# Router logits of a mixture-of-experts layer: from TensorE matmuls to products on VectorE and sums on ScalarE

## The chip, the cores and the metric

The kernel runs on one core of one Trainium2 chip. The core has five engines with an instruction queue each, and each queue is worked off in order: TensorE (PE, matmuls; its weight loads are listed as PEld), VectorE (DVE), ScalarE (ACT), GpSimd (POOL) and SyncE (SP, which here only issues transfers and reads table entries). Time is device time of one execution in microseconds. The kernel before takes 2452.55 us, the median of 3 runs (2449.38 to 2454.42).

## The reference

The inputs are a batch of 4 with 64 channels, 512 time steps and 64 variables; the model width is D = 256, and 16384 tokens come out. All is float32.

```python
h = tok(x, W)                    # patches of 16, stride 8, FFT, one linear map to D
x1 = layernorm(h)
a  = layernorm(x1)
q, k, v = a @ Wq.T + bq, a @ Wk.T + bk, a @ Wv.T + bv
mem_t = decay * mem_{t-1} + k_t * v_t        # a scan along the tokens
x2 = x1 + q * mem
h  = h + x2 + relu(layernorm(x2) @ W1.T + b1) @ W2.T + b2
tokens = layernorm(h)            # the expert layer's input
logits = tokens @ router_w.T     # 8 experts: the part that is changed
rw, re = top_k(softmax(logits), 2);  rw = rw / rw.sum(-1)
h = h + tokens + sum_e combine[:, e] * (gelu(tokens @ w1[e] + b1[e]) @ w2[e] + b2[e])
```

## The kernel before

Tokens go through in 32 blocks of 512, each held as four groups of 128 tokens (TT = 4) on the 128 partitions. The main loop runs over periods; period i works at three blocks at once: `new` (block i: embedding, layernorms, q/k/v and the scan), `mid` (block i-1: the MLP) and `old` (block i-2: routing). Between their parts stand up to four slots; a slot is one step over the queue of expert tiles of 256 gathered tokens, taken while more than 12 tiles (LEFT) wait, and in the last periods while any wait. The two last periods have no `new`, the very last no `mid` either; what is left of the tiles follows after them.

A period's program, in the order in which it is written: embed's first part (L258, ScalarE's copy into `ms` at L262); features2 of mid (transposes of `zz`, L213, and ScalarE's copies with scale, L221); the first half of embed (L269, VectorE's sum into `h` at L276, statistics at L184 and L185); features3 of old (transposes of `tok`, copies L215); embed's second half, then rstd on GpSimd (L191 to L196) and `zz` and `z` on VectorE (L200); slot A; eight mlp_in (L229 on TensorE, relu on ScalarE at L343), the first four with a group of old's logits after each (L385); slot B and choose after the fourth; features1 of new before the eighth; place, take and the differences `xd` of the next block (L246, L247); retention for two halves of the features (per half three products L229, `ks` on ScalarE at L298, and `kv`, the scan and `ret` on VectorE at L300 to L313); slot C; mlp_out for the first half (L351, VectorE L358); residual (transposes of `ret` L323, VectorE L326, rstd on GpSimd, `zz` at L200, two additions to `h` at L332 and L333); slot D; mlp_out for the second half, which ends with rstd on GpSimd, `tok` on VectorE (L200) and the addition to `h` at L365.

choose finds the two best experts of each token in some 13 tiny VectorE instructions (L404 to L420) and a power on GpSimd (L422). place counts, by two matmuls (L429), where each token's rows go, and writes them with eight indirect DMAs from GpSimd (L450). take turns the counts into tables of tiles, which SP reads. In a slot, TensorE transposes the tile after the next (turn, L572), multiplies one (enter, L581) and finishes the one before (leave, L598). ScalarE copies `xT` (L574) and applies gelu (L589, two instructions). VectorE makes `y` (L607 to L614), and GpSimd adds its rows into the output in DRAM by two indirect DMAs (L618); the adds of a tile wait for those of the tile before.

The order is written out by hand: on TensorE, VectorE, ScalarE and SP the instructions stand in the order of the program (`manual_schedule`); on GpSimd, too, they come out in that order here. The PSUM pools set further bounds: `p_mm` has four buffers and holds, one after another, the outputs of transposes into features, mlp_in, q, k, v, turn and enter; `p_tm` has three, for embed, residual, leave and mlp_out.

Of the kernel before, what the change touches and what calls it, by code (L numbers as in the profile page):

```python
# [12 lines left out]
F32 = mybir.dt.float32  # L13
I32 = mybir.dt.int32
AF = mybir.ActivationFunctionType
# [14 lines left out]
def vit_tower_kernel(  # L30
# [17 lines left out]
    D = wtok.shape[1]  # L48
    C = P // 2
    H = w1.shape[1]  # L50
    E = rw.shape[1]
    KD, KH = D // P, H // P
    J = STRIDE // 2
    TT = 4
# [69 lines left out]
    nc.sync.dma_start(out=w1_sb, in_=w1.rearrange("(k p) h -> p k h", p=P))  # L124
    w2_sb = const.tile([P, KH, D], F32)
    nc.sync.dma_start(out=w2_sb, in_=w2.rearrange("(k p) d -> p k d", p=P))
    rw_sb = const.tile([P, KD, E], F32)
    nc.sync.dma_start(out=rw_sb, in_=rw.rearrange("(k p) e -> p k e", p=P))
    mb2_sb = const.tile([P, D], F32)
    nc.sync.dma_start(out=mb2_sb, in_=mb2.partition_broadcast(P))  # L130
    rc = const.tile([P, 2, P], F32)
# [102 lines left out]
    class Block:  # L234
# [139 lines left out]
                    channel_multiplier=2,  # L374
                )

        def features3(self):
            self.tokT = one.tile([P, KD, BLK], F32, name="tokT")
            to_features(self.tokT, self.tok)

        def logits(self, t):
            if t == 0:
                self.lg = p_sm.tile([P, TT, E], F32, name="sm")
            for k in range(KD):
                nc.tensor.matmul(  # L385
                    self.lg[:, t, :],
                    lhsT=self.tokT[:, k, ts(t, P)],
                    rhs=rw_sb[:, k, :],
                    start=k == 0,
                    stop=k == KD - 1,  # L390
                )

        def choose(self):

            ps = self.lg
            shape = [P, TT, E]

            def wide(a):
                return a.unsqueeze(2).to_broadcast(shape)

            lg = small.tile(shape, F32, name="lg")
            top = small.tile([P, TT], F32, name="top")
            first_key = self.tok[:, :, FIRST]
            nc.vector.tensor_copy(lg, ps)  # L404
            nc.vector.tensor_reduce(top, lg, AX.X, ALU.max)
            nc.vector.tensor_tensor(lg, lg, wide(top), ALU.subtract)
            key = small.tile(shape, F32, name="key")
            self.oh = oh = small.tile([P, 2, TT, E], F32, name="oh")
            nc.vector.scalar_tensor_tensor(key, lg, 0.0, key0, ALU.is_equal, ALU.mult)
            nc.vector.tensor_reduce(first_key, key, AX.X, ALU.max)  # L410
            nc.vector.tensor_tensor(oh[:, 0], key, wide(first_key), ALU.is_equal)
            nc.vector.scalar_tensor_tensor(lg, oh[:, 0], -3.0e38, lg, ALU.mult, ALU.add)
            second = small.tile([P, TT], F32, name="second")
            nc.vector.tensor_reduce(second, lg, AX.X, ALU.max)
            nc.vector.tensor_tensor(key, lg, wide(second), ALU.is_equal)
            nc.vector.tensor_tensor(key, key, key0, ALU.mult)
            nc.vector.tensor_reduce(top, key, AX.X, ALU.max)
            nc.vector.tensor_tensor(oh[:, 1], key, wide(top), ALU.is_equal)
            self.both = small.tile(shape, F32, name="both")
            nc.vector.tensor_tensor(self.both, oh[:, 0], oh[:, 1], ALU.add)  # L420
            self.ex = small.tile([P, TT], F32, name="ex")
            nc.gpsimd.tensor_tensor(self.ex, euler, second, ALU.pow)  # L422
# [238 lines left out]
    with tc.manual_schedule(engines=MANUAL):  # L661
        xs[1] = load_x(1)
        blocks[0].differences(xs.pop(0))
        for i in range(NB + 2):
            new = blocks[i] if i < NB else None
            mid = blocks[i - 1] if 1 <= i <= NB else None
            old = blocks[i - 2] if i >= 2 else None
            embed = new.embed() if new else iter(())
            next(embed, None)
            if mid:  # L670
                mid.features2()
            next(embed, None)
            if old:
                old.features3()
            next(embed, None)
            slot(LEFT if new else 0)
            for m in range(KH):
                if mid:
                    mid.mlp_in(m)
                if old and m < TT:  # L680
                    old.logits(m)
                if m == TT - 1:
                    slot(LEFT if new else 0)
                    if old:
                        old.choose()
                if new and m == KH - 2:
                    new.features1()
            if not mid:
                slot(0)
            if old:  # L690
                take(old.i + 1, old, old.place())
            if i + 1 < NB:
                blocks[i + 1].differences(xs.pop(i + 1))
                if i + 2 < NB:
                    xs[i + 2] = load_x(i + 2)
            if new:
                for m in range(KD):
                    new.retention(m)
                slot()
            if mid:  # L700
                mid.mlp_out(0)
            if new:
                new.residual()
                slot()
            if mid:
                mid.mlp_out(1)
            if mid and not new:
                slot(0)
                slot(0)
# [84 lines left out]
```

## Time and profile before

| | |
|---|---|
| median of 3 runs | 2452.55 us |
| the profiled execution's own time | 2448.38 us |
| its span, first to last instruction | 2446.4 us |
| busy time: PE, DVE, POOL, ACT | 2298.4, 1347.3, 930.1, 556.7 us |
| mean granted TensorE clock | 0.979 |

The page counts an engine as busy while it executes; waits on semaphores are not busy time. The timeline lists instructions with start, duration, engine and line; brackets give the idle time ahead of an instruction and what ended it. A label such as `mm<-hT,w_sb` reads output first, then inputs. A float32 matmul shows as two records of matmul, so that a group of TensorE can list twice the count of the program.

### The profile page before, as it was taken

Reading aid. Unit: us, or ns where it says so; the run is one execution under the profiler, and the core shown is the slowest. Engines: PE = TensorE matmul, PEld = TensorE weight load, DVE = VectorE, ACT = ScalarE, POOL = GpSimd, SP = SyncE. Lnnn points to the kernel's source line nnn. Section 1 sums busy time; section 2 is a strip of 40 time slices with the busy share of each in tenths; the row PEclk is TensorE's granted clock in tenths of the full one; section 3 lists DMA queues with packets and bytes.
Section 4 is the critical chain, followed back from the end, with each engine's and each line's share of the span. In section 5 each row is a group of like instructions: output and inputs, shape, how many; then the busy total and the mean of one; then the engine's idle time right before and its main releaser. Section 6 shows DMA issues by size and latency. Waiting matters only on the chain. (4 is left out here: it accounts for less than half of the span.)

```text
span 2446.4 us, 29049 instructions
## 1 busy us (share of the span) xinstructions
PE 2298.4 (94%) x9740; PEld 1687.8 (69%) x9740; DVE 1347.3 (55%) x4111; ACT 556.7 (23%) x952; POOL 930.1 (38%) x845
## 2 busy tenths in 40 slices
PE   3999999999999999999999999999999999986673
PEld 2677666777777777777777777777777777665553
DVE  6566665565655555655555556555555665533221
ACT  0122222222222222222222222222222222221221
POOL 0022222344444334444443344444433444335444
PEclk8999999999999999999999999999999999998887
DMA  4021121333344343333443433334334333347674
GB/s 140 18 79 59 56 105 64 98 89 102 109 122 116 103 110 101 89 102 109 122 113 105 112 101 89 102 109 122 111 107 111 102 90 85 91 106 208 168 182 86
DMA packets 128181, 256.44 MB, mean 105 GB/s; under 512 B 14497, under 2 KB 88097, under 8 KB 123937
## 3 DMA queue, kind: packets, MB, share of 16 engines
q1 hardware_dynamic: 76864, 185.09, 23.3%
q0 software_dynamic: 51168, 69.50, 15.3%
q8 instruction: 77, 1.26, 0.2%
q14 instruction: 72, 0.58, 0.1%
HBM read 164.04 MB, written 90.50 MB: 104 GB/s over the span
## 5 line engine op out<-in xcount | busy, mean ns | idle before, releaser
L618 POOL DMA_INDIRECT out<-y,xg x270 | 426.1, 1578 | 587.6 <-DVE y L614 386.9
L229 PE MATMUL mm<-hT,w_sb 128*128 128x512 f32 x1024 | 478.3, 600 | 0.0
L351 PE MATMUL tm<-w_sb,aT 128*128 128x256 f32 x2048 | 453.0, 379 | 0.0
L351 PEld LDWEIGHTS tm<-w_sb,aT 128*128 128x128 f32 x2048 | 388.5, 190 | 54.9 <-issue 2.4
L450 POOL DMA_INDIRECT xbuf<-tok,row x256 | 314.4, 1228 | 238.1 <-DVE whole L506 161.5
L229 PE MATMUL mm<-hT,wqkv_sb 128*128 128x512 f32 x768 | 338.1, 596 | 0.1
L612 DVE TENSOR_TENSOR y<-tm,w 128x512 f32<-128x512 f32 x135 | 93.3, 691 | 382.8 <-PE tm L598 226.9
L229 PEld LDWEIGHTS mm<-hT,w_sb 128*128 128x128 f32 x1024 | 184.6, 190 | 158.4 <-issue 155.4
L581 PE MATMUL mm<-xT,w 128*128 128x256 f32 x1080 | 275.9, 401 | 3.5 <-DVE ret L313 2.3
L191 POOL TENSOR_SCALAR rstd<-mv 128x4 f32<-128x4 f32 x96 | 37.1, 387 | 635.8 <-DVE mv L185 635.8
L343 ACT ACTIVATE aT<-mm,vec 128x512 f32<-128x512 f32 x256 | 175.9, 687 | 395.2 <-PE mm L229 392.6
L229 PEld LDWEIGHTS mm<-hT,wqkv_sb 128*128 128x128 f32 x768 | 143.9, 191 | 169.6 <-issue 154.1
L598 PE MATMUL tm<-w,ge 128*128 128x256 f32 x1080 | 258.4, 383 | 0.0
L269 PE MATMUL tm<-weff,xd 128*128 128x256 f32 x1024 | 233.4, 382 | 8.5 <-DVE xd L246 8.5
L581 PEld LDWEIGHTS mm<-xT,w 128*128 128x128 f32 x1080 | 206.2, 201 | 34.6 <-DVE ret L313 9.2
L598 PEld LDWEIGHTS tm<-w,ge 128*128 128x128 f32 x1080 | 209.1, 194 | 29.9
L269 PEld LDWEIGHTS tm<-weff,xd 128*128 128x128 f32 x1024 | 191.1, 192 | 32.7 <-DVE xd L246 8.9
L574 ACT COPY xT<-mm 128x512 f32<-128x512 f32 x135 | 79.0, 585 | 531.3 <-PE mm L572 528.2
L589 ACT ACTIVATE ge<-mm,w 128x256 f32<-128x256 f32 x270 | 113.1, 470 | 182.7 <-PE mm L581 157.2
L572 PE MATMUL mm<-ident,xg 128*128 128x128 f32 x540 | 85.1, 282 | 64.9 <-DMA xg<-xbuf 64.8
L258 PE MATMUL tm<-wsum,xb 128*128 128x256 f32 x512 | 118.3, 385 | 25.8 <-ACT wsum L115 25.8
L358 DVE TENSOR_TENSOR h<-tm,h 128x512 f32<-128x512 f32 x64 | 44.0, 687 | 174.8 <-PE tm L351 174.8
(112 smaller groups left out, 2277.2 us busy)
## 6 DMA issues: line engine op xcount, KB each, us to landing
w<-in_wex SPq DMA_DIRECT2D x135, 641.5 KB
xg<-xbuf SPq DMA_DIRECT2D x135, 260.0 KB
xb<-in_x SPq DMA_DIRECT2D x32, 1040.0 KB
out<-h SPq DMA_DIRECT2D x32, 512.0 KB
out<-y,xg POOLq DMA_INDIRECT x270
xbuf<-tok,row POOLq DMA_INDIRECT x256
xbuf<-none SPq DMA_DIRECT2D x8, 260.0 KB
w_sb<-in_w SPq DMA_DIRECT2D x2, 1024.0 KB
```

The source lines that it names most:

```text
L229: nc.tensor.matmul(ps, lhsT=w[:, k, ts(m, P)], rhs=rhs[:, k, :], start=k == 0, stop=k == KD - 1)
L258: nc.tensor.matmul(ps[:, u, :], lhsT=od[:, j, ts(u, P)], rhs=wsum[:, j, :], start=j == 0, stop=j == J - 1)
L269: nc.tensor.matmul(ps[:, i, :], lhsT=xd[:, i, j, ts(u, P)], rhs=weff[:, i * J + j, :], start=j == 0, stop=j == J - 1,)
L343: nc.scalar.activation(self.aT[:, m, :], ps, AF.Relu, bias=vec[:, MB1 + m : MB1 + m + 1])
L351: nc.tensor.matmul(ps[:, i, :], lhsT=self.aT[:, k, ts(u * 2 + i, P)], rhs=w2_sb[:, k, :], start=k == 0, stop=k == KH - 1,)
L450: write = nc.gpsimd.indirect_dma_start(out=xbuf, out_offset=bass.IndirectOffsetOnAxis(ap=row[:, c, t : t + 1], axis=0), in_=self.tok[:, t, :],
L572: nc.tensor.transpose(ps[:, k, c, :], self.xg[:, c, ts(k, P)], ident)
L581: nc.tensor.matmul(ps[:, m, :], lhsT=self.w[:, k * D + m * P : k * D + (m + 1) * P], rhs=self.xT[:, k, :], start=k == 0, stop=k == KD - 1,)
L589: nc.scalar.activation(self.ge[:, m, :], ps[:, m, :], AF.Gelu, bias=self.w[:, 5 * D + m : 5 * D + m + 1])
L598: nc.tensor.matmul(ps[:, c, :], lhsT=self.ge[:, k, ts(c, P)], rhs=w[:, (2 + k) * D : (3 + k) * D], start=k == 0, stop=k == KD - 1,)
L612: nc.vector.tensor_tensor(y, ps, w[:, 4 * D : 5 * D].unsqueeze(1).to_broadcast([P, 2, D]), ALU.add)
L618: add = nc.gpsimd.indirect_dma_start(out=out, out_offset=bass.IndirectOffsetOnAxis(ap=self.xg[:, c, NUMBER : NUMBER + 1].bitcast(I32), axi ...
```

## The change

The router's matrix `rw_sb` is no longer held as features on partitions (128 x 2 x 8) but as its eight rows, copied to every partition (128 x 8 x 256). features3 is gone, and with it the transposes of `tok` and their copies. logits becomes a generator of eight parts. A part takes one of the four token groups and four of the eight experts: VectorE multiplies the four rows with the group's tokens into `prod` (two buffers), and ScalarE runs four activations (identity) over 256 elements each, in place, whose sums over the row are the logits, in SBUF instead of PSUM.

The parts are spread over the period: one after the first half of embed, one after the second; one after each of mlp_in 1, 3, 5 and 7 (counted from 0); one ahead of each half of retention. choose comes after retention, then slot C, then place and take. The differences of the next block come ahead of retention as before, but now also ahead of choose and place; the load of the input after it (load_x) comes after take. Lines of the new kernel below choose lie three further down than in the old (place's matmuls L432, row DMAs L453, `xT` L577, gelu L592, adds L621).

```diff
-    rw_sb = const.tile([P, KD, E], F32)
-    nc.sync.dma_start(out=rw_sb, in_=rw.rearrange("(k p) e -> p k e", p=P))
+    rw_sb = const.tile([P, E, D], F32)
+    nc.sync.dma_start(out=rw_sb, in_=rw.rearrange("e d -> (e d)").partition_broadcast(P).rearrange("p (e d) -> p e d", e=E))
...
-        def features3(self):
-            self.tokT = one.tile([P, KD, BLK], F32, name="tokT")
-            to_features(self.tokT, self.tok)
-
-        def logits(self, t):
-            if t == 0:
-                self.lg = p_sm.tile([P, TT, E], F32, name="sm")
-            for k in range(KD):
-                nc.tensor.matmul(
-                    self.lg[:, t, :],
-                    lhsT=self.tokT[:, k, ts(t, P)],
-                    rhs=rw_sb[:, k, :],
-                    start=k == 0,
-                    stop=k == KD - 1,
-                )
+        def logits(self):
+
+            self.lg = small.tile([P, TT, E], F32, name="lg")
+            for t in range(TT):
+                for e in range(0, E, E // 2):
+                    prod = two.tile([P, E // 2, D], F32, name="prod")
+                    nc.vector.tensor_tensor(
+                        prod,
+                        rw_sb[:, e : e + E // 2, :],
+                        self.tok[:, t : t + 1, :D].to_broadcast([P, E // 2, D]),
+                        ALU.mult,
+                    )
+                    for j in range(E // 2):
+                        nc.scalar.activation(
+                            prod[:, j, :],
+                            prod[:, j, :],
+                            AF.Identity,
+                            accum_out=self.lg[:, t, e + j : e + j + 1],
+                        )
+                    yield
...
             embed = new.embed() if new else iter(())
+            logits = old.logits() if old else iter(())
             next(embed, None)
             if mid:
                 mid.features2()
             next(embed, None)
-            if old:
-                old.features3()
+            next(logits, None)
             next(embed, None)
+            next(logits, None)
             slot(LEFT if new else 0)
             for m in range(KH):
                 if mid:
                     mid.mlp_in(m)
-                if old and m < TT:
-                    old.logits(m)
+                if m % 2:
+                    next(logits, None)
                 if m == TT - 1:
                     slot(LEFT if new else 0)
-                    if old:
-                        old.choose()
                 if new and m == KH - 2:
                     new.features1()
             if not mid:
                 slot(0)
+            if i + 1 < NB:
+                blocks[i + 1].differences(xs.pop(i + 1))
+            if new:
+                for m in range(KD):
+                    next(logits, None)
+                    new.retention(m)
+            for _ in logits:
+                pass
+            if old:
+                old.choose()
+            if new:
+                slot()
             if old:
                 take(old.i + 1, old, old.place())
-            if i + 1 < NB:
-                blocks[i + 1].differences(xs.pop(i + 1))
-                if i + 2 < NB:
-                    xs[i + 2] = load_x(i + 2)
-            if new:
-                for m in range(KD):
-                    new.retention(m)
-                slot()
+            if i + 2 < NB:
+                xs[i + 2] = load_x(i + 2)
             if mid:
                 mid.mlp_out(0)
```

## The prediction

> **What bounds the kernel now.** I read the page's first two parts, then the busy time by stretches, then the timeline of one period, then the end of the timeline. Page, busy time and slices:
>
> ```profile
> PE 2298.4 (94%) x9740; PEld 1687.8 (69%) x9740; DVE 1347.3 (55%) x4111; ACT 556.7 (23%) x952; POOL 930.1 (38%) x845
> ...
> PE   3999999999999999999999999999999999986673
> ```
>
> The average hides two regimes: a full TensorE until slice 36, a slack one after. Busy time by stretches (us, busy time and count of PE, PEld, DVE, ACT, POOL; clock; DMA share; GB/s):
>
> ```profile
> 1230.00:1300.00 70.00, 69.85 (x302) 51.44 (x301) 40.91 (x128) 16.96 (x29) 28.67 (x25) 1.00 0.40 107
> ...
> 2200.00:2446.00 246.00, 152.68 (x658) 124.53 (x657) 60.98 (x209) 44.38 (x94) 114.18 (x77) 0.83 0.68 163
> ```
>
> In the body one period (one turn of the main loop) lasts 69.95 us: the ms copy starts at 1162.99 and at 1232.94. TensorE works in all of it, so the period is its program. ScalarE and VectorE have room, on average. In the last 230 us the chain that ended last is expert tiles, one after another, each 6.8 us (issues of L618 at 2422.63, 2428.98, 2435.80): the order of their adds into the output.
>
> Lines of the timeline that the sum leans on (start, us, engine, line; in brackets idle time before and its releaser):
>
> ```profile
> 1223.29 0.23 POOL L191 TENSOR_SCALAR rstd<-mv 128x4 f32<-128x4 f32 x1 [7.60 <-DVE mv L185]
> 1245.85 1.38 DVE L200 TENSOR_SCALAR zz<-h,mv,rstd 128x256 f32<-128x256 f32 x4 [2.36 <-POOL rstd L196]
> 1256.31 0.84 ACT L589 ACTIVATE ge<-mm,w 128x256 f32<-128x256 f32 x2 [1.14 <-DMA xb<-in_x]
> 2144.50 2.21 PE L213 MATMUL mm<-ident,tok 128*128 128x128 f32 x8 [5.28 <-DVE tok L200]
> 2147.35 3.51 PE L581 MATMUL mm<-xT,w 128*128 128x256 f32 x8
> 2150.70 1.89 PE L598 MATMUL tm<-w,ge 128*128 128x256 f32 x8
> ```
>
> First: GpSimd is idle 7.6 us before residual's rstd; today the eight row DMAs are long over. Second: rstd of a new block comes 2.36 us after its statistics. Third: two 128x256 activations back to back, 0.42 us each. The last three: after a gap of 5.28 us TensorE works at half pace (L581 3.51 us, in the body 1.89) and is back at pace 6.2 us after the restart.
>
> **The change, part by part.** Removed from TensorE per block: transposes of tok (weight loads at 1236.85 and then 1237.83: 0.98 us) and four pairs of logits (L229 groups 2.16 us apart with them, 1.72 without: 4 x 0.44). That is 2.7 us a period; the body would go to 67.3 us, 81 us less over the 30 periods with logits. Removed from ScalarE: two tokT copies, 1.07 us.
>
> Added: VectorE, eight products of 128x1024, 1.21 us each (the xd subtraction L246 has this shape): 9.7 us. ScalarE, 32 activations of 128x256 with a sum. No row shows a summing activation. Lower bound 0.42 us, the third line above, if the sum costs nothing. Upper bound: L343 takes 687 ns for 512 elements and L589 470 for 256, so 253 ns are fixed; a sum written out as if by an instruction of its own adds that, on top of a lone 0.47: 0.72. I take 0.42 + 0.25 = 0.67, 2.7 us for a part of four, since each sum goes to an address of its own; the ends stay for the range. By totals all fits: ScalarE 16.96 - 1.07 + 21.4 = 37.3 of 67, VectorE 40.91 + 9.7 = 50.6. But the engines work in order, and the change ties them in a loop. Three places:
>
> 1. Part 2 sits on ScalarE ahead of slot A's xT, and needs prod 2, which VectorE makes after the new block's z. The mm pool has four buffers: turn, enter, mlp_in 0 and 1 fill them, and mlp_in 2 waits for that xT.
> 2. Parts 7 and 8 stand ahead of the two ks copies, prod 8 behind retention 0, choose behind retention 1. TensorE reaches place's matmuls (L432) with one slot (3.9 us) as cover.
> 3. choose and place come after retention, so the ex, slot C's adds and the eight row DMAs stand on GpSimd right ahead of residual's rstd.
>
> The loop in a full period, from the end of choose to the next end of choose (us; rows from the timeline 1198 to 1276):
>
> - VectorE y of slot C, 1.9 (L607 to L614, 1248.44 to 1250.13); its two adds on GpSimd, 3.8 with gaps (1250.16 to 1253.69); eight row DMAs at 0.96 and 0.30 between them, 10.6: at 16.3. Residual's statistics are ready at 13.5, earlier.
> - rstd 1.5 (1223.2 to 1224.68), zz and two adds to h 3.7 (to 1228.37), y of slot D 1.7: at 23.2. Its adds and the rstd of mlp_out, until tok starts, 5.0 (1230.07 to 1235.05): 28.2. tok and h 2.55: 30.75.
> - Embed half 1 into h with statistics 1.9 (1237.60 to 1239.49), prod 1 1.2, half 2 1.9, rstd 2.4, zz and z 2.7 (1245.85 to 1248.52), prod 2 1.2: at 42.05.
> - ScalarE part 2 2.7, xT 0.6: at 45.35. TensorE could have begun mlp_in 2 at 38.0 (choose's end + 19.4 to the period's first matmul, + 18.6 to mlp_in 2), so it stands 7.4 us, more than the 5.28 above, and restarts at half pace: mlp_in 2 and 3 take 3.45 each, slot B 3.9, mlp_in 4 and 5 1.73 each; the relu of 5 is out at 60.4. At full pace ScalarE's own queue would give 57.2.
> - ScalarE: parts 5, 6, 7 (8.1), relu 6 and 7 (1.4), hT (1.5), ks of retention 0 (0.7): 72.1.
> - VectorE retention 0 3.2 (ks end to ret end), prod 8 1.2, part 8 2.7, ks 0.7, retention 1 3.2, choose 2.65: **85.8**.
>
> So 85.8 us against 69.95: the tensor engine's saving is off the path. Without slots (the early periods) the same links without the slots' y, adds, xT and ge, and with place's 3.4 ahead of the rows, give 74; before, ms copies are 54.1 apart (127.62, 181.74).
>
> Of the clock: the Trainium skill, page "TensorE: Matmul & The Clock Gate", section "What's actually happening", says the array runs at half rate after an idle window of about 3.4 us and needs as long at work to return. The row above shows the half pace but 6.2 us of it. By the page the restart would cost about 1.7 us a period, not the 3.2 I add, and the total would be 36 us less; the row decides.
>
> Tail. The number of expert steps after the last mlp_out goes from 33 to 34, since take now stands behind slot C: +6.8. In the first period without a new block ScalarE runs eight parts before choose: from that period's first TensorE work to place 45.9 us by the same rows, 33.6 before (2138.2 to 2171.8): +12.3. The last block's parts run beside five tiles of the add chain (5 x 6.8 us against 8 x 2.7): nothing; if the chain waited, at most 10 us.
>
> At no cost: the two xd subtractions (2.4 us), now ahead of prod 7 on VectorE, since ScalarE reaches part 7 some 20 us later by the list; the router rows, now 1 MB instead of 8 KB on SP at the start, needed only in the third period (the next in the queue, mb2, in residual 0, some 30 us later); load_x of the block after next, which moves on SP behind slot C's tile loads and VectorE's take: issued at 1250.00 now, its data are read one period after (xd at 1271.80, 69.95 later), and moves by some 20 us of that. Were that cover gone, xd and retention would wait.
>
> Sum over the profiled execution (span 2446.4, time 2448.4, 4 us under the median of the runs): 4 early periods of about +20 = 80; two mixed ones (57.3 and 62.2 before, about 77 and 80 after) = 38; 24 full ones at +15.85 = 380; tail 19. Span 2963; with the 2 us around it and rounding, I say **2963 us**.
>
> **The rivals.**
> - *The gain comes through* (other side): TensorE stays the bound at 67.3, 2448 - 81 + 6.8 = 2374. For it: the totals. Against: the loop must lose 15.9 us to come level at 69.95. At a full clock it is 82.6, of which seven parts in the chain are 18.9; a sum would have to cost 0.22 us each, while 256 elements alone take 0.217. Chance 0.03; no change 0.01.
> - *Sums are free and the clock stays full*: 0.42 each; loop 77.3, early periods 67: 24 x 7.4 + 6 x 13 + 13 = +269, 2717. Half way there (one of the two) 2830 to 2890. For it: at full pace the granted clock reads 1.00 in the body. Chance 0.28 in all.
> - *The rows don't hold rstd*: residual's statistics at 13.5 then lead, 2.8 us less over 30 periods: 2880. For it, the 7.6 us of idle GpSimd; against, its queue is in order. Chance 0.08, inside the former's spread.
> - *It is longer still*: row DMAs at 12.2 us as from 1198.82 to 1211.03 (+48), sums at 0.72 (+42), a second restart at half pace before mlp_out (2 us, +48): 3100 with all. Chance 0.10 beyond 3050.
> - My forecast's own spread, 2890 to 3050: 0.50.
>
> **How the numbers follow.** Range 2700 (free sums, full clock) to 3100 (all three extras); a tenth lies on each side. Faster or slower means by over 0.2%, about what a measurement of this kernel can tell: faster 0.03, same 0.01, slower 0.96.
>
> **What would show it.** Right: periods of 80 to 88 us between ms copies; TensorE idle some 7 us before the third mlp_in with ScalarE xT as releaser; then L229 at half pace; ScalarE idle before the second part of sums with VectorE prod as releaser; GpSimd's rstd starting straight after the eighth row DMA; granted clock clearly under 1.00. Wrong: periods near 67 with TensorE full; or summing activations of 0.4 us, or of over 0.8.

## The result and the profile after

The changed kernel takes 2695.99 us, the median of 4 runs (2694.48 to 2700.97), against 2452.89 us (2449.38 to 2454.42) for the kernel before in the same comparison. The ratio is 1.0997, with a 95% interval of 1.0978 to 1.1016: slower, by 243 us. The profiled execution took 2697.18 us with a span of 2695.4 us and a granted clock of 0.936, against 0.979 before.

The page of the changed kernel: busy time, TensorE's slices and its granted clock.

```profile
PE 2329.2 (86%) x8972; PEld 1653.7 (61%) x8972; DVE 1634.7 (61%) x4335; ACT 904.8 (34%) x2936; POOL 924.3 (34%) x845
...
PE   4988888899999999998998999899999999975774
...
PEclk8999889999999999999999999999999999987887
```

TensorE executes 768 fewer records, as the diff says, and yet is busy for longer (2329.2 us against 2298.4): part of its work ran at half pace. The slices that were all 9 now hold many 8s. VectorE and ScalarE stand at 61% and 34%, so neither is full on average.

Busy time by stretches, first 600 us of the body of the kernel before, then the same 600 us after with the two stretches that answer to those shown of before (one long period, and the last 246 us). Columns: window, its length, then busy time and count of PE, PEld, DVE, ACT and POOL; clock; DMA share; GB/s.

```profile
1300.00:1900.00 600.00, 598.83 (x2573) 439.25 (x2572) 347.60 (x1086) 149.06 (x254) 244.76 (x215) 1.00 0.40 109
```

```profile
1300.00:1900.00 600.00, 554.04 (x2169) 392.12 (x2168) 391.93 (x1048) 221.42 (x727) 225.24 (x198) 0.96 0.37 99
...
1500.00:1578.00 78.00, 71.10 (x284) 50.93 (x283) 52.73 (x147) 28.46 (x93) 29.49 (x26) 0.98 0.36 96
...
2449.00:2695.00 246.00, 146.06 (x608) 119.19 (x608) 61.04 (x205) 45.71 (x106) 112.41 (x75) 0.81 0.64 154
```

TensorE, which worked without a break before, now stands idle for 46 of 600 us and works more slowly in part of the rest (granted clock 0.96), while ScalarE has 378 of 600 us free. No engine is full: what was lost is time in which engines wait for each other. The last 246 us, by contrast, look much as before (146 us of TensorE, where it was 153). TensorE's waits in the changed kernel name the places (engine, what waited, on whom; us in total, times, longest):

```profile
PE sm L432 <- DVE both L423: 100.6, 32, 12.0
PE mm L229 <- ACT xT L577: 94.7, 25, 5.5
PE mm L575 <- DMA xg<-xbuf: 62.2, 24, 15.9
...
PE mm L229 <- ACT aT L343: 23.2, 6, 3.9
```

The first is place, which waits for choose. The second is mlp_in 2, which waits for the copy `xT` behind part 2. Both are places that the prediction named. The third lies behind 2400 us, in the last periods and what follows, and stood at 64.8 us before.

Now the timeline around them (start, us, engine, line; in brackets the idle time before and its releaser), in the order of the rows shown of before:

```profile
1517.75 0.96 POOL L453 DMA_INDIRECT xbuf<-tok,row  x1 [0.30 <-issue]
1518.12 0.18 DVE L185 BATCH_NORM_AGGREGATE mv<-st 128x2 f32<-128x6 f32 x1
1518.79 0.23 POOL L191 TENSOR_SCALAR rstd<-mv 128x4 f32<-128x4 f32 x1
...
1542.88 1.22 DVE L383 TENSOR_TENSOR prod<-rw_sb,tok 128x1024 f32<-128x1024 f32 x1
1544.19 0.42 ACT L390 ACTIVATE prod<-prod 128x256 f32<-128x256 f32 x1 [6.27 <-DVE prod L383]
1545.80 0.56 ACT L577 COPY xT<-mm 128x512 f32<-128x512 f32 x1
1546.41 3.70 PE L229 MATMUL mm<-hT,w_sb 128*128 128x512 f32 x8 [3.31 <-ACT xT L577]
...
1562.37 0.41 ACT L390 ACTIVATE prod<-prod 128x256 f32<-128x256 f32 x1
1562.68 0.19 ACT L390 ACTIVATION_READ_ACCUMULATOR prod<-prod 128x1 f32 x1
1562.77 0.40 ACT L390 ACTIVATE prod<-prod 128x256 f32<-128x256 f32 x1
...
1578.26 0.63 PE L432 MATMUL sm<-both,rc 128*128 128x32 f32 x4 [1.80 <-DVE both L423]
1578.72 8.84 PE L351 MATMUL tm<-w_sb,aT 128*128 128x256 f32 x32
...
1592.24 7.07 PE L351 MATMUL tm<-w_sb,aT 128*128 128x256 f32 x32
...
1621.16 6.55 PE L229 MATMUL mm<-hT,w_sb 128*128 128x512 f32 x8 [3.29 <-ACT xT L577]
...
1656.32 7.15 PE L351 MATMUL tm<-w_sb,aT 128*128 128x256 f32 x32
...
1698.76 5.31 PE L229 MATMUL mm<-hT,w_sb 128*128 128x512 f32 x8 [4.98 <-ACT xT L577]
```

Five things are to be read here. First, GpSimd's rstd no longer has 7.6 us of idle time ahead of it: it starts 0.08 us after the eighth row DMA's issue ends (1518.71), and its statistics had been complete for 0.49 us (1518.30). In about every third period, where the first mlp_out takes 7.15 us (1656.32) and not 8.84, the statistics are complete 2.16 us ahead of rstd: there only the row DMAs hold it. Second, part 2 begins on ScalarE when prod 2 is done, after 6.27 us of idle time, and `xT` stands behind it. Third, TensorE stands still until that `xT`: for 3.3 us in two of three periods, for 5.0 in the third (1698.76). Fourth, a summing activation starts every 0.40 us (1562.37, 1562.77): the read-out of the sum, 0.19 us, runs while the next activation has already begun, so a part of four takes 1.6 us. Fifth, half pace shows in two places: mlp_out takes 8.84 us after place's gap and 7.07 us a slot later, and the same pair of mlp_in takes 3.70 us in one period, 6.55 in the next and 5.31 in the one after it.

By the distances between ms copies (29 of them lie from the third copy, at 127.62 us before and 129.15 after, to the last, at 2072.30 and 2288.90), the difference of 249 us between the two spans is made up so:

| stretch | before | after | difference |
|---|---|---|---|
| up to the third ms copy | 127.6 | 129.2 | +1.5 |
| six early periods (few or no slots) | 336.0 | 408.0 | +72 |
| 23 full periods | 23 x 69.95 | 23 x 76.16 | +143 |
| last ms copy to the end | 374.1 | 406.5 | +32 |

Most of the full periods take 78.05, 74.75 and 75.95 us in turn.

### The profile page after: what moved, and what is told of

Its sections match the earlier page's. It is cut to its first block, busy times and chain, and to the rows that moved or that the text cites. A ratio compares the mean times of both kernels' runs of the same rounds, so it can differ in the third digit from the quotient of the medians.

```text
span 2695.4 us, 29696 instructions
## 1 busy us (share of the span) xinstructions
PE 2329.2 (86%) x8972; PEld 1653.7 (61%) x8972; DVE 1634.7 (61%) x4335; ACT 904.8 (34%) x2936; POOL 924.3 (34%) x845
## 5 line engine op out<-in xcount | busy, mean ns | idle before, releaser
L621 POOL DMA_INDIRECT out<-y,xg x270 | 487.5, 1805 | 651.6 <-DVE y L617 503.3
L229 PE MATMUL mm<-hT,w_sb 128*128 128x512 f32 x1024 | 510.6, 647 | 117.9 <-ACT xT L577 94.7
L390 ACT ACTIVATE prod<-prod 128x256 f32<-128x256 f32 x1024 | 411.2, 407 | 531.4 <-DVE prod L383 531.4
L351 PE MATMUL tm<-w_sb,aT 128*128 128x256 f32 x2048 | 500.4, 407 | 0.0
L351 PEld LDWEIGHTS tm<-w_sb,aT 128*128 128x128 f32 x2048 | 418.2, 206 | 65.0 <-issue 0.5
L229 PEld LDWEIGHTS mm<-hT,w_sb 128*128 128x128 f32 x1024 | 208.2, 209 | 363.4 <-issue 206.9
L229 PE MATMUL mm<-hT,wqkv_sb 128*128 128x512 f32 x768 | 336.1, 594 | 0.9 <-ACT hT L221 0.9
L383 DVE TENSOR_TENSOR prod<-rw_sb,tok 128x1024 f32<-128x1024 f32 x256 | 306.1, 1215 | 29.9 <-ACT prod L390 29.9
L453 POOL DMA_INDIRECT xbuf<-tok,row x256 | 248.4, 970 | 103.8 <-issue 68.3
L229 PEld LDWEIGHTS mm<-hT,wqkv_sb 128*128 128x128 f32 x768 | 146.2, 191 | 185.5 <-issue 154.0
L425 POOL TENSOR_TENSOR ex<-euler,second 128x4 f32<-128x4 f32 x32 | 33.9, 1058 | 604.9 <-DVE second L417 604.9
L577 ACT COPY xT<-mm 128x512 f32<-128x512 f32 x135 | 77.6, 575 | 484.2 <-PE mm L575 256.6
L390 ACT ACTIVATION_READ_ACCUMULATOR prod<-prod 128x1 f32 x1024 | 196.1, 191 | 0.0
L300 DVE SCALAR_TENSOR_TENSOR kv<-mm,vec,ks 128x512 f32<-128x512 f32 x64 | 48.1, 751 | 241.7 <-ACT ks L298 225.5
```

Source lines behind the costliest of these rows:

```text
L229: nc.tensor.matmul(ps, lhsT=w[:, k, ts(m, P)], rhs=rhs[:, k, :], start=k == 0, stop=k == KD - 1)
L351: nc.tensor.matmul(ps[:, i, :], lhsT=self.aT[:, k, ts(u * 2 + i, P)], rhs=w2_sb[:, k, :], start=k == 0, stop=k == KH - 1,)
L383: nc.vector.tensor_tensor(prod, rw_sb[:, e : e + E // 2, :], self.tok[:, t : t + 1, :D].to_broadcast([P, E // 2, D]), ALU.mult,)
L390: nc.scalar.activation(prod[:, j, :], prod[:, j, :], AF.Identity, accum_out=self.lg[:, t, e + j : e + j + 1],)
L453: write = nc.gpsimd.indirect_dma_start(out=xbuf, out_offset=bass.IndirectOffsetOnAxis(ap=row[:, c, t : t + 1], axis=0), in_=self.tok[:, t, :],
L577: nc.scalar.copy(self.xT, ps.rearrange("p k c q -> p k (c q)"))
```

## The experiments

The main theory is the prediction's loop: choose comes late, place, adds and row DMAs follow it, rstd, tok and prod 2 follow these, and through ScalarE's queue they reach mlp_in 2, the ks copies and the next choose. The rivals are that the products and sums simply cost too much of an engine (occupancy), that lateness of place alone does it, or that TensorE's gaps can be taken one at a time. Each experiment was timed beside the kernel before, whose median was 2449 to 2450 us in each.

### The late places alone

The kernel before, with choose, place, take and load_x moved to where the change has them; logits stay TensorE matmuls.

```diff
                     slot(LEFT if new else 0)
-                    if old:
-                        old.choose()
...
-            if old:
-                take(old.i + 1, old, old.place())
             if i + 1 < NB:
                 blocks[i + 1].differences(xs.pop(i + 1))
-                if i + 2 < NB:
-                    xs[i + 2] = load_x(i + 2)
             if new:
                 for m in range(KD):
                     new.retention(m)
+            if old:
+                old.choose()
+            if new:
                 slot()
+            if old:
+                take(old.i + 1, old, old.place())
+            if i + 2 < NB:
+                xs[i + 2] = load_x(i + 2)
```

> The logits stay on TensorE as in the kernel before; only the places of choose, place, take and load_x are those of the changed kernel (behind retention and slot C). Loop theory (the period is the chain choose, row DMAs, rstd, embed, and back to choose, so the place of choose costs by itself): place's matmuls wait about 2.3 us for choose in a full period and 6 us in an early one, mlp_out then runs at half pace for a while (1.8 us more): periods about 74, time about 2600. Occupancy theory (the sums and products on ScalarE and VectorE cost by their own time): nothing is added here, 2450 to 2460.

Measured: 2531.43 us, ratio 1.0328 (1.0311 to 1.0345). TensorE's waits:

```profile
PE mm L572 <- DMA xg<-xbuf: 73.9, 24, 16.6
PE sm L429 <- DVE both L420: 31.0, 30, 4.2
...
PE mm L213 <- DVE tok L200: 18.2, 24, 7.4
```

It fell between the two forecasts. A full period is 71.24 us, 1.3 more than before, so the loop without products is no longer than that, and shorter than I had said (74); place's gap is 0.26 us in a full period, where no sums stand ahead of ks, and 4.15 us in an early one, where no slot covers it. The early periods grew to 60 or 61 us, and the stretch from the last ms copy to the end grew by 14 us. So the move of choose and place by itself costs 82 us, a third of the whole, some 30 of them (23 x 1.3) in the full periods. It cannot be the whole.

### Part 2 behind slot A

```diff
             next(embed, None)
-            next(logits, None)
             slot(LEFT if new else 0)
+            next(logits, None)
             for m in range(KH):
```

> Changed kernel with part 2 of the logits moved behind slot A, so that ScalarE copies xT first. Loop theory: the 3.3 us gap ahead of mlp_in 2 goes; part 2 now stands ahead of relu 0, for which slot B's turn waits about 1.6 us; period 76.2 to 74.6, time about 2645. Gap theory (each gap of TensorE is a cost of its own): the 3.3 us and the half pace after it in a quarter of the periods are saved, about 2590. Occupancy theory: 2696 unchanged.

Measured: 2643.82 us, ratio 1.0779 (1.0760 to 1.0798), a mean full period of 73.91 us. As the loop said (2645). TensorE's waits:

```profile
PE sm L432 <- DVE both L423: 98.0, 32, 9.6
...
PE mm L575 <- ACT aT L343: 63.2, 24, 3.6
```

Nearly all of the 94.7 us of waiting on `xT` are gone; in their place TensorE waits for the relus behind part 2, 2.6 us a period in the mean (1.58 us in one period, some 3.25 in the next two). One reordered line is worth 52 us, but the wait moves one link on and does not vanish.

### Matmuls that fill the gap at place

The changed kernel with five matmuls, whose results nobody uses, ahead of place's own. They end the idle time after which mlp_out ran at half pace.

```diff
-            ps = p_sm.tile([P, 2, TT, E], F32, name="sm")
+            sm = p_sm.tile([P, 512], F32, name="sm")
+            ps = sm[:, : 2 * TT * E].rearrange("p (i t e) -> p i t e", i=2, t=TT)
+            for i in range(5):
+                nc.tensor.matmul(sm[:, 256:], lhsT=ident, rhs=w2_sb[:, i, :], start=True, stop=True)
```

> Changed kernel with five idle matmuls of 128x256 (1.9 us) on TensorE ahead of place's, into an unused part of their PSUM tile: TensorE waits for choose as long as before but without a gap, so mlp_out behind it should run at full pace (6.9 instead of 8.7 us). They compute nothing that is used. Gap or clock theory: 1.8 us less in 24 periods, about 2650. Loop theory: rstd of residual is set by the eighth row DMA (15.3 us after choose) as much as by mlp_out's statistics (14.9), so the saved time comes back as a longer gap ahead of mlp_in 2 (5.1 instead of 3.3): 2685 to 2700.

Measured: 2707.97 us, ratio 1.1047 (1.1029 to 1.1066), above the range of either forecast. Timeline of TensorE in a period:

```profile
1508.63 2.32 PE L433 MATMUL sm<-w_sb,ident 128*128 128x256 f32 x10
1510.79 0.53 PE L435 MATMUL sm<-both,rc 128*128 128x32 f32 x4
1511.15 7.15 PE L351 MATMUL tm<-w_sb,aT 128*128 128x256 f32 x32
...
1553.51 5.18 PE L229 MATMUL mm<-hT,w_sb 128*128 128x512 f32 x8 [4.90 <-ACT xT L580]
```

mlp_out got back to pace (7.15 us), and what it gained came back as a longer wait for `xT`: 4.90 us instead of 3.31. That is what the loop says and what the theory of separate gaps does not: the moment of mlp_in 2 is set by the chain on the other engines, and work that TensorE does faster before it only waits longer: the third mlp_in starts 43.0 us after the end of choose in both kernels. That the kernel is even 12 us slower lies behind that wait, in the chain itself: with the gap at 4.9 us in every period, the pair of mlp_in after it takes 5.83 us in the mean of the 23 full periods, against 5.13 in the changed kernel, which is 16 us in all.

### Shorter sums

The changed kernel with sums over 64 of the 256 elements. The other elements are left out of the logits.

```diff
                         nc.scalar.activation(
-                            prod[:, j, :],
-                            prod[:, j, :],
+                            prod[:, j, :64],
+                            prod[:, j, :64],
```

> Changed kernel whose sums run over 64 of the 256 products, so the router's logits are incomplete (other experts are chosen); the products are unchanged. A sum gets 0.16 us shorter. Loop theory: only parts 2 and 8 lie in the loop, 1.3 us of a period, about 2655. Occupancy theory: all 32 sums count, 5.1 us of a period, about 2540. If the read-out of the sum then sets the pace (0.19 us, now hidden), the gain is smaller.

Measured: 2652.38 us, ratio 1.0822 (1.0803 to 1.0841), full period 74.96 us. A sum now starts every 0.24 us instead of 0.40, so 0.64 us per part, and ScalarE lost 5 us of work per period; yet the period is only 1.2 us shorter. Occupancy (2540) is out. The gap at place shrank, and in exchange the gap ahead of mlp_in 2 grew, with half pace after it (a pair at full pace takes 3.60 us). TensorE, then ScalarE and VectorE behind it:

```profile
1515.18 6.31 PE L229 MATMUL mm<-hT,w_sb 128*128 128x512 f32 x8 [4.32 <-ACT xT L577]
1548.03 0.63 PE L432 MATMUL sm<-both,rc 128*128 128x32 f32 x4 [0.71 <-DVE both L423]
```

```profile
1533.17 0.69 ACT L343 ACTIVATE aT<-mm,vec 128x512 f32<-128x512 f32 x1 [0.50 <-PE mm L229]
...
1536.67 0.75 DVE L300 SCALAR_TENSOR_TENSOR kv<-mm,vec,ks 128x512 f32<-128x512 f32 x1 [4.23 <-PE mm L229]
```

The time came out as the loop theory said (2655), but not for its reason, that parts 2 and 8 alone count. From prod 2 to the end of `xT` the period lost the 0.64 us of part 2, and behind ks 0.33 us of part 8's. From `xT` to ks, with three parts in it, it lost only 0.16 of 1.92 us: the slower pair of mlp_in took 1.1 back (6.26 us in the mean, against 5.13), and TensorE itself now sets the pace there. The last relu waits 0.50 us for it, so part 5 counts for nothing, and `kv` starts 0.34 us after `ks` is ready, released by TensorE's product.

### Parts 7 and 8 both ahead of retention

```diff
             if new:
+                for _ in logits:
+                    pass
                 for m in range(KD):
-                    next(logits, None)
                     new.retention(m)
```

> Changed kernel with parts 7 and 8 both ahead of retention, so that prod 8 no longer waits behind the first half's scan and part 8 not behind ks. Loop theory: the first ks comes 1.6 us later, but choose 1.9 us earlier: period 76.2 to 74.3, time about 2640. Occupancy theory: 2696 unchanged.

Measured: 2650.22 us, ratio 1.0824 (1.0806 to 1.0842), full period 74.94 us. The last products and sums no longer alternate with the two halves of retention, and place's gap falls from 1.80 to 0.27 us. The work is the same, only its place in two queues is another: 46 us less, near the loop's 2640 and far from the 2696 of occupancy.

### Place behind the first mlp_out

The other direction: place, take and load_x one step later, behind the first half of mlp_out.

```diff
                 slot()
+            if mid:
+                mid.mlp_out(0)
             if old:
                 take(old.i + 1, old, old.place())
             if i + 2 < NB:
                 xs[i + 2] = load_x(i + 2)
-            if mid:
-                mid.mlp_out(0)
```

> Changed kernel with place, take and load_x moved one step later, behind the first half of mlp_out. TensorE then no longer waits for choose. Gap theory: the 1.8 us gap and the half pace behind it go, about 2610. Loop theory: the eight row DMAs start 4 to 5 us later, ahead of residual's rstd on GpSimd, and the loop gets longer by that: 2780 to 2820.

Measured: 2819.59 us, ratio 1.1516 (1.1497 to 1.1535), full period 81.94 us. TensorE no longer waits at place in the full periods, where the changed kernel lost 1.80 us in each, and the kernel is 124 us slower. The waits:

```profile
PE mm L229 <- ACT xT L577: 175.0, 25, 8.6
PE tm L351 <- DVE z L326: 79.7, 25, 3.2
```

Covering TensorE's wait by delaying place lengthens the loop, and the loop is what counts: the eighth row DMA's issue ends 19.8 us after choose, not 15.3, and every link behind it moves with it.

### Products on top of the kernel before

The kernel before with the eight products and 32 sums added at the change's places, over constant rows and with results that nobody uses; TensorE still makes the logits, and choose and place stand where they stood.

```diff
+    rows_sb = const.tile([P, E, D], F32)
+    nc.gpsimd.memset(rows_sb, 0.5)
...
                 old.features3()
+            next(parts, None)
             next(embed, None)
+            next(parts, None)
...
+                if m % 2:
+                    next(parts, None)
...
             if new:
                 for m in range(KD):
+                    next(parts, None)
                     new.retention(m)
```

> Kernel before, with the eight products and their sums added at the places of the changed kernel (the rows hold a constant and the sums are used by nothing); TensorE still makes the logits, and choose and place stay where they were. Loop theory: part 2 still stands ahead of xT and costs a gap of about 2.4 us ahead of mlp_in 2, with 0.7 us at slot C: periods about 73, time 2520 to 2550. Together with the late place alone (2531 measured) that is less than the changed kernel's loss, since there the two delays lie in one chain. Occupancy theory: the whole loss is here, 2700 or more, as the removed TensorE work is back.

Measured: 2756.06 us, ratio 1.1250 (1.1231 to 1.1268), full period 80.47 us. A miss for the loop (2520 to 2550), and inside what occupancy had said (2700 or more), so the number alone speaks for occupancy; the waits do not. The `xT` wait was there as expected, 2.29 us in a period; the larger wait was another, ahead of the second half of retention. TensorE, then VectorE and ScalarE ahead of it:

```profile
1502.39 1.99 PE L231 MATMUL mm<-hT,w_sb 128*128 128x512 f32 x4 [2.29 <-ACT xT L597]
...
1530.54 5.40 PE L231 MATMUL mm<-hT,wqkv_sb 128*128 128x512 f32 x8 [4.21 <-ACT ks L300]
```

```profile
1524.69 1.21 DVE L248 TENSOR_TENSOR xd<-xb 128x1024 f32<-128x1024 f32 x1
1525.83 1.20 DVE L249 TENSOR_TENSOR xd<-xb 128x1024 f32<-128x1024 f32 x1
1526.96 1.21 DVE L401 TENSOR_TENSOR prod<-rows_sb,tok 128x1024 f32<-128x1024 f32 x1
```

```profile
1528.21 0.42 ACT L408 ACTIVATE prod<-prod 128x256 f32<-128x256 f32 x1 [6.23 <-DVE prod L401]
1529.82 0.67 ACT L300 ACTIVATE ks<-mm,vec 128x512 f32<-128x512 f32 x1
```

Here product 7 stands on VectorE behind place, the tables of take (1521.29 to 1524.7) and both `xd`; part 7 waits for it with ScalarE idle for 6.23 us, and ks, which frees PSUM for TensorE, waits behind part 7. I had not counted what would stand ahead of product 7 when place stays early. That it is order and not load shows in the next experiment, which carries the same products and sums.

### Choose one period later

If the loop is the cause, it must open when choose has a whole period of slack. Three things change at once here, the place of choose, the places of the parts, and buffers and LEFT. The changed kernel, with choose, place and take one period later at the places of the kernel before; parts after mlp_in 1, 3, 5 and 7 and the last four behind slot C, none ahead of `xT` and none ahead of ks; `tok` in three buffers, LEFT at 8, one more turn of the loop.

```diff
-                self.tok = two.tile([P, TT, RW], F32, name="tok")
+                self.tok = three.tile([P, TT, RW], F32, name="tok")
...
-    LEFT = 12
+    LEFT = 8
...
-        for i in range(NB + 2):
+        for i in range(NB + 3):
...
+            late = blocks[i - 3] if i >= 3 else None
...
-            next(logits, None)
             next(embed, None)
-            next(logits, None)
             slot(LEFT if new else 0)
...
+                if m == TT + 1 and late:
+                    late.choose()
...
+            if late:
+                take(late.i + 1, late, late.place())
...
                 for m in range(KD):
-                    next(logits, None)
                     new.retention(m)
-            for _ in logits:
-                pass
-            if old:
-                old.choose()
-            if new:
                 slot()
-            if old:
-                take(old.i + 1, old, old.place())
...
+            for _ in range(4):
+                next(logits, None)
```

> Products and sums kept, but choose, place and take of a block come one period later, at the places of the kernel before (choose after the fifth mlp_in, place behind mlp_in, ahead of retention); four parts of the logits stand behind mlp_in 1, 3, 5, 7 and four behind slot C; the token tile has three buffers and a slot is taken from 9 waiting tiles instead of 13. Loop theory: nothing in a period waits for a part of the same period, so TensorE is the bound again, less the removed 2.7 us: periods 67.3 to 68, time 2375 to 2400. Occupancy theory (the work added to ScalarE and VectorE costs by its size): no better than the changed kernel less the gap at place, 2600 or more.

Measured: 2384.32 us, ratio 0.9740 (0.9724 to 0.9756): faster than both kernels. Its busy time by stretches and its page:

```profile
1300.00:1900.00 600.00, 598.71 (x2465) 435.83 (x2464) 444.15 (x1183) 248.01 (x807) 273.05 (x222) 1.00 0.41 110
```

```profile
PE 2217.6 (93%) x8972; PEld 1602.6 (67%) x8972; DVE 1634.3 (69%) x4335; ACT 911.8 (38%) x2936; POOL 993.4 (42%) x845
```

TensorE is full again, with as many instructions as in the changed kernel (8972) and 112 us less busy time at a clock of 1.00 in the body; ScalarE and VectorE do the same products and sums and have room. A full period is 67.33 us, so the 2.7 us that the change takes from TensorE are real. The same work in another order, with a third buffer for `tok` and the lower LEFT, takes 312 us less. How much of it belongs to choose and how much to the parts that no longer stand ahead of `xT` and ks, this run alone does not divide.

### Longer sums

Was the prediction off because the chain was wrong, or because one size in it was? The changed kernel with sums over 576 overlapping elements, so that the logits hold other numbers.

```diff
+                    flat = prod.rearrange("p e d -> p (e d)")
                     for j in range(E // 2):
+                        long = flat[:, j * 149 : j * 149 + 576]
                         nc.scalar.activation(
-                            prod[:, j, :],
-                            prod[:, j, :],
+                            long,
+                            long,
```

> Changed kernel whose four sums of a part run over 576 elements each instead of 256 (overlapping stretches of the same product tile, so the logits are other numbers and other experts are chosen): a sum should take 0.67 us, the size that the prediction gave it, instead of the measured 0.40. If the prediction's chain was right and mostly the size of the sum was wrong, the period goes from 76.2 to 82 to 84 and the time to 2850 to 2900, near what was predicted, with parts 2 to 8 on ScalarE in the chain. If only parts 2 and 8 lie in the chain, as the short sums suggest for small sizes, the period goes to 78.3 and the time to 2760.

Measured: 2953.92 us, ratio 1.2055 (1.2035 to 1.2075), full period 84.16 us. ScalarE, then TensorE:

```profile
1535.77 0.68 ACT L392 ACTIVATE prod<-prod 128x576 f32<-128x576 f32 x1 [4.77 <-DVE prod L383]
...
1538.88 0.56 ACT L579 COPY xT<-mm 128x512 f32<-128x512 f32 x1
...
1564.37 0.68 ACT L392 ACTIVATE prod<-prod 128x576 f32<-128x576 f32 x1
1564.96 0.18 ACT L392 ACTIVATION_READ_ACCUMULATOR prod<-prod 128x1 f32 x1
1565.18 0.68 ACT L392 ACTIVATE prod<-prod 128x576 f32<-128x576 f32 x1
```

```profile
1539.49 6.62 PE L229 MATMUL mm<-hT,w_sb 128*128 128x512 f32 x8 [6.50 <-ACT xT L579]
...
1574.47 1.99 PE L586 MATMUL mm<-xT,w 128*128 128x256 f32 x8 [3.75 <-ACT ks L298]
```

This has to be read with care. The total comes out beside the predicted 2963, above both forecasts of the run, and the gap ahead of mlp_in 2 (6.50 us) beside the predicted 7.4. But the sums came out longer than meant: the next activation overwrites part of what this one reads, and the starts are 0.81 us apart, not 0.67. From its first activation to the start of `xT`, part 2 takes 3.11 us (1535.77 to 1538.88), where it took 1.61 (1544.19 to 1545.80). What the run does show is the slope: a part became longer by 1.5 us, the period by 8.0. Of these, 0.9 are the pair of mlp_in, slower behind the longer gap (5.99 us in the mean, against 5.13); the other 7.1 are 4.8 parts of 1.5, and the prediction's chain holds five (parts 2, 5, 6, 7 and 8). By the same run, parts of the predicted 2.7 us would give 2696 + (1.1/1.5) x 258 = 2885 us, an estimate.

## Why the prediction was right or wrong

**The direction and the mechanism were right.** The gain on TensorE is real (a full period of 67.33 us with the loop opened, 67.3 predicted) and was lost because the change ties the engines into a loop through choose. The waits are where they were said to be, and lengthening or shortening the loop moved the time as it should in most of the experiments. The late places alone, the products on top, the filler and the longer sums fell outside what the loop theory had said, and the shorter sums came out at its number for another reason. Occupancy, gap by gap, and lateness alone fail in at least one each by far more.

**The size was wrong by 267 us** (2963 predicted, 2696 measured). 222 of them lie in the 23 full periods (85.8 us predicted, 76.16 measured). The chain of the prediction beside the period from 1503.44 to 1578.20 us, from the end of choose to the next end of choose:

| link | predicted | measured |
|---|---|---|
| choose to the end of the eighth row DMA's issue | 16.3 | 15.3 |
| to the end of prod 2 | 25.75 | 25.4 |
| to the end of `xT` (part 2) | 3.3 | 2.3 |
| to the end of ks of retention 0 (parts 5, 6, 7) | 26.75 | 19.9 |
| to the end of choose (part 8) | 13.7 | 12.0 |
| sum | 85.8 | 74.8 |

**The step that failed is the price of a summing activation**, taken as 0.67 us between bounds of 0.42 and 0.72. It is 0.40. The reason given for the surcharge (each sum goes to an address of its own, which costs another fixed share) was half right: there is such an instruction, of 0.19 us, but the next activation starts before it ends. Five parts in the chain, each 1.6 instead of 2.7 us, are 5.4 of the 9.6 us by which a full period was too long, 124 us over 23 periods. For the whole kernel the longer sums put it at some 190 us (2885 against 2696, an estimate). The shorter sums gave back less (44 us for 0.16 us a sum), since below 0.40 TensorE is the next to bind.

**The second step is the clock after the gap.** I took half pace for 3.2 us in each period, from a row after a gap of 5.28 us. The gap was 3.3, 3.3 and 5.0 us here, not 7.4, and after these three the pair of mlp_in took 3.70, 6.55 and 5.31 us against 3.60 at full pace. From choose to choose these periods take 74.76, 77.6 and 76.4 us, and but for some 0.1 us they differ only in the link with that pair. The mean period is 1.4 us above the period in the table, so 1.8 us were too much, 41 us in 23 periods. Here the row that I let decide was further from the truth than the rule that I weighed against it: the Trainium skill, page "TensorE: Matmul & The Clock Gate", section "What's actually happening", would have put 1.7 us, an estimate worked out from the page's window of about 3.4 us at half rate. Its statement that the window in which the gate watches is free-running, so that the moment of a switch depends on where in it the work begins, also fits what the trace shows: after equal gaps of 3.3 us, 3.70 us in one period and 6.55 in the next.

**The rest, smaller.** The row DMAs ended 1.0 us earlier (the eight took 9.9 us, not 10.6, and what precedes them 5.4, not 5.7). They held rstd up by 0.4 us in two of three periods, where mlp_out at half pace had made the statistics late, and by 2.1 us in the third. So in most periods the rival "the rows don't hold rstd" was nearly level with my case, and of the 2.8 us between the two, 2.1 were there in one period of three. Some 1.4 us of the 9.6 are spread over links without one cause. In the early periods I predicted +118 us and measured +72: 46 of the 267. There the loop without slots is 66 to 68 us, not 74. By the prediction's own links five parts of 1.6 instead of 2.7 us would make it 68.6, so most of this is the price of the sums once more; the rest stays open. From the last ms copy to the end I had 19, and 16 for the last full period, 35 in all: measured +32. That agreement is luck: from the last ms copy to the first TensorE work of the period without a new block it was 8.1 us and not 16, from there to place 5.2 and not 12.3, in the stretch to the end of mlp_out 1.8, and behind it 17.3 and not 6.8. The one further expert step was there (36 for 35); what makes the other 10 us behind mlp_out stays open.

**The rivals.** "Sums are free and the clock stays full", 2717, is the nearest in total, and the first half of it is what the trace shows. Its loop, 77.3, is close to the measured 76.16, in part by luck: the clock does not stay full (0.96 in the body), and the period with the pair at 3.70 us, nearly full pace, takes 74.75. "The gain comes through", 2374, was the right price for a kernel without the loop, as the 2384 us of the experiment show, but not for this one.

**What my list of signs said.** Periods of 80 to 88 us and a gap of some 7 us did not come. ScalarE xT as releaser, ScalarE waiting for prod ahead of part 2, rstd straight behind the eighth row DMA and a clock under 1.00 did; L229 at half pace came in two of three periods. And the last sign named as wrong, activations of 0.4 us, came: with it the prediction was off where it said that it would be.

**What stays open.** In full periods the loop is in force, but TensorE is close behind it: from 1546.41 to 1572 us it works without a break, so that a further cut of the sums saves little. That is why the shorter sums gave 1.2 us a period where five parts of 0.64 would be 3.2. The experiments do not add up to 243 us one by one, nor can they: in a loop each saving is limited by the next link.

## What to carry to other kernels

Work moved from a full engine to engines with room is free only if it does not stand, in their in-order queues, ahead of something that the full engine waits for; here the sums cost time through the copies out of PSUM (`xT`, ks) that stood behind them, and none that shows once they stood elsewhere (67.33 us a period). Before pricing such a change, follow the result of the moved work around the loop until it meets itself, count which links carry the new work, and ask whether a period of slack can be put into it: the same work, with choose one period later and no part ahead of `xT` and ks, turned +10% into -2.6%. And a price without a row of its own is to be given as its bounds and carried through the loop as often as it occurs: an error of 0.27 us in an activation was counted 20 times in each period.

## What the runs showed of the hardware

- A ScalarE activation with a sum over its row is two instructions, 407 and 191 ns in the mean over 1024, and the second overlaps with the next activation: 0.40 us from start to start for 128x256, 0.24 for 128x64. The group lines of the changed kernel:

```profile
L390 ACT ACTIVATE prod<-prod 128x256 f32<-128x256 f32 x1024 | 411.2, 407 | 531.4 <-DVE prod L383 531.4
...
L390 ACT ACTIVATION_READ_ACCUMULATOR prod<-prod 128x1 f32 x1024 | 196.1, 191 | 0.0
```

- In the longer sums, where the next activation writes over what this one reads, the overlap is gone: 0.81 us from start to start with activations of 0.68. That the overwriting and not the length is the reason was not tested.
- TensorE fell to half pace after a gap of 1.80 us, with place's few small matmuls behind it: mlp_out took 8.84 us in two of three periods and 7.15 in the third, always after the same gap. The clock fell only when TensorE was at work again: it reads 0.71 from 1578.3 to 1580.3 us and 0.50 in the 2 us behind. The Trainium skill, page "TensorE: Matmul & The Clock Gate", section "What's actually happening", speaks of an idle window of about 3.4 us; here less was enough, in some periods. When five idle matmuls filled the gap, mlp_out took 7.15 us.
- Half pace in mlp_out cost the period nothing, because the loop runs elsewhere at that point; half pace in the pair of mlp_in, which lies in the loop, did cost (from choose to choose 74.76 us with 3.70, 77.6 with 6.55). After the two mlp_out at 8.84 us the gap ahead of mlp_in 2 is 3.3 us, after the one at 7.15 us it is 4.98 us (1698.76), and mlp_in 2 starts 43.0 us after choose in all three.
